# A graph layer's step on TensorE: counts of a slice ahead of placing, begun at group 28 instead of 31

## The chip, the cores and the metric

The kernel runs on one core of a Trainium2 chip. The metric is the device time of one execution in microseconds (us), the median of several runs. Five engines work side by side from queues of their own: TensorE (PE, with its weight loads as PEld), VectorE (DVE), ScalarE (ACT), GpSimd (POOL) and SyncE (SP, which issues DMAs).

## The reference

One layer of a graph network over 12500 nodes of 256 features, with 200000 edges sorted by their destination:

```
h   = relu(layernorm(x))                       # 12500 x 256
agg = segment_sum(h[src], dst)                 # 200000 edges
z   = (1 + eps_gin) * h + agg
t   = relu(batchnorm(z @ W1 + b1, g1, bt1))    # 12500 x 512
out = x + relu(batchnorm(t @ W2 + b2 + h, g2, bt2))
```

## The kernel before, in words

The edges are cut into tiles of 128 and the tiles into 131 groups of 12 (`GT`). One iteration of the loop at L951 is a *step* and belongs to one group; 126 steps run there, the last five groups after it. What a step does:

- **Fetching.** POOL's `gather` (L592) issues 12 indirect DMAs, each fetching the 128 source rows of a tile, four groups ahead of the sums that read them. There are four buffers, so the gather of a group waits until the sums of the fourth fetched group before it have been read. Groups below `LEAD` = 30 fetch rows of `x`, and their layer norm is done on the fly: `look` on DVE (L477), `scale` on DVE (L496, L498), `relus` on ACT (L504). Later groups fetch finished rows from `h_one`.
- **Summing.** DVE compares destinations with a ramp (`oh`, `edges`, L645) and PE's `sums` (L677) multiplies one-hot by rows, 12 tiles per group, two matmul records a tile in the trace. Two groups that follow each other share one PSUM tile (`ps`). `hold` (L731) copies a group's sum out as `zs` two steps later: on ACT below group 30, on DVE from there.
- **Placing.** PE's `put` (L744) spreads the sum of group i-3 to its columns; it writes a PSUM tile `pz2` from the pool `ps_z`, which has two. DVE's `add` (L759) of group i-4 adds such a tile to `zc` and so frees it.
- **Slices.** When a chunk of 512 nodes is complete, the first product follows in four *slices*, one a step: PE's `slice_of` (L769). With `apart` its result goes into `ps_z` too, so that places and slices take the two tiles in turn; without, into another pool (`next_ph`). In the next step `take` reads it on DVE (L780), copies it (L786: ACT up to step 30, then DVE), and sends it to `t_tab`.
- **Counting.** Ten groups (`COUNTED`: 41, 50, ..., 122) are not fetched. For each, the sum over its edges is made from all of `h` and a matrix of counts, in 13 *strips*: DVE marks (`mark`, L868, one step ahead, with an SP DMA of 1 MB of `h_one`, L874), PE counts (`count_of`: `count`, L887, 12 bf16 matmuls, and ACT's copy L899), and PE's `weigh` (L917, 8 matmuls) multiplies the strip before by its rows. `prepare` (L847 on) makes what the marks need, once, at the end of the step before `BEGIN`. The table `plan` gives one or two of the 130 strips to each step from `BEGIN` on: after n such steps int(`RATE` * n) strips are done.

Order on each engine is the order in which the code is written (a manual schedule); the framework adds semaphores where tiles are reused. In a step PE's list `works` is spread evenly between the 12 tiles of the sums. At a counted step, which has no sums, the list runs by itself.

Of the kernel before, what the change touches and what calls it, by code (L numbers as in the profile page):

```python
# [23 lines left out]
LEAD = 30  # L24
# [5 lines left out]
COUNTED = tuple(range(41, 131, 9))  # L30
WINDOWS = 4
BLOCKS = 8
BEGIN = 31
RATE = 1.6


COPIES = 2
# [6 lines left out]
def kernel(  # L44
# [23 lines left out]
    NCH = -(-N // CH)  # L68
# [86 lines left out]
    def slot(ga, t):  # L155
        return slots(ga, t)[:, 0, :]
# [231 lines left out]
    def fast():  # L388
# [24 lines left out]
        with ExitStack() as fs:  # L413
# [15 lines left out]
            with ExitStack() as es:  # L429
# [99 lines left out]
                def look_chunk(g):  # L529
                    look(((0, R, xts[g]),), -(-len(parts[g]) // 2), "c", g)  # L530
# [74 lines left out]
                def wait_for(i, eng):  # L605

                    if i in arrival:
                        eng.wait_ge(*arrival.pop(i))
                        return True
# [44 lines left out]
                def sum_place(i):  # L654
                    if not halves:
                        pair = ps_s.tile([P, 2, D], F32, name="ps")
                        halves.extend((pair[:, 1, :], pair[:, 0, :]))
                    return halves.pop()

                def sums(i, among=()):  # L660

                    if i in COUNTED:
                        for work in among:
                            work()
                        return
                    t0, n = groups[i]
                    ga, oh = gathered.pop(i), ohs.pop(i)
                    waited = wait_for(i, nc.tensor)
                    ps = sum_place(i)
                    order = list(reversed(range(n)))  # L670
                    at = {(k + 1) * n // (len(among) + 1): work for k, work in enumerate(among)}
                    for k, j in enumerate(order):
                        if k in at:
                            at[k]()
                        rows = left if t0 + j == full_tiles else P
                        lhsT, rhs = oh[:rows, j, :], slot(ga, j)[:rows]
                        part = nc.tensor.matmul(ps, lhsT=lhsT, rhs=rhs, start=(j == order[0]), stop=(j == order[-1]))  # L677
                        if waited:
                            behind(i, part)
                            waited = False  # L680
                    summed[i] = ps
# [79 lines left out]
                def slice_of(c, f, apart=False):  # L761

                    n = chunks[c][1] * R
                    if apart or c == NCH - 1 and f >= 2:
                        ph = ps_z.tile([P, DC, WIDE], F32, name="pz2").rearrange("p d w -> p (d w)")
                    else:
                        ph = next_ph()
                    for d in range(DC):
                        nc.tensor.matmul(  # L769
                            ph[:, :n], lhsT=w1s[:, d, f * P : (f + 1) * P],  # L770
                            rhs=zc[c][:, d, :n], start=(d == 0), stop=(d == DC - 1),
                        )
                    slices[c, f] = ph
                    if f == HC - 1:
                        del zc[c]
# [50 lines left out]
                plan, strips, turns_of = {}, [(k, s) for k in range(NC) for s in range(NS)], 0  # L826
                for i in range(BEGIN, NG - CLOSE):
                    if i not in COUNTED:
                        turns_of += 1
                        upto = min(int(turns_of * RATE), len(strips))  # L830
                        done = sum(len(v) for v in plan.values())
# [119 lines left out]
                for i in range(NG - CLOSE):  # L951
                    before = added
                    if next_of(i) is not None:
                        gather(next_of(i))
                    if 0 < i <= NCH:
                        turn(i - 1)
                    if i + 1 < LEAD:
                        scale("g", i + 1)
                    if i < NCH:
                        scale("c", i)  # L960
                    edges(i + FRONT)
                    if i >= 2:
                        spots(i - 2)
                        hold(i - 2)
                    if i + 1 < LEAD:
                        relus(gathered[i + 1], GT, gathered[i + 1], "g", i + 1)
                    if i < NCH:
                        h_chunk(i)
                    if i + 2 < LEAD:
                        look(gathered[i + 2], GT // 2, "g", i + 2)  # L970
                        root("g", i + 2)
                    if i + 1 < NCH:
                        look_chunk(i + 1)
                        root("c", i + 1)
                    for c, f in taken:
                        if i > LEAD:
                            take(c, f, nc.vector.tensor_copy, nc.sync)
                        else:
                            take(c, f)
                    while added <= i - 4:  # L980
                        add(added)
                        added += 1
                    if 0 < i <= NCH:
                        turn_out(i - 1)
                    if i < NCH:
                        h_rows(i)
                    for c in scales.get(i, ()):
                        z_scale(c)

                    def puts():  # L990
                        if i >= 3:
                            put(i - 3)

                    while last(whole) < before:
                        queue += [(whole, f) for f in range(HC)]
                        whole += 1
                    taken = queue[:1]
                    queue = queue[1:]

                    def slice_ups():  # L1000
                        for c, f in taken:
                            slice_of(c, f, i >= LEAD)

                    works = [puts, slice_ups]
                    for one in plan.get(i, ()):
                        works.append(functools.partial(count_of, *one))
                        if strips.index(one):
                            works.append(functools.partial(weigh, *strips[strips.index(one) - 1]))
                        if one == strips[-1]:
                            works.append(functools.partial(weigh, *one))  # L1010
                    sums(i, works)
                    if i + 1 == BEGIN:
                        prepare()
                    for one in plan.get(i + 1, ()):
                        mark(*one)
                    for c in loads.get(i, ()):
                        z_load(c)
# [604 lines left out]
```

## Time and profile before

| | |
|---|---|
| median of 3 runs | 2024.14 us (2023.56 to 2026.66) |
| the profiled execution | 2024.22 us, span 2022.4 us |
| mean granted TensorE clock | 0.952 |
| PE busy | 1779.5 us (88%) |
| DVE busy | 1259.6 us (62%) |
| ACT busy | 569.5 us (28%) |
| POOL busy | 1440.0 us (71%) |
| DMA | 462.70 MB, mean 229 GB/s |

A timeline row gives the start of a run of like instructions and its length, the engine, the line, what is written and read, and in brackets the idle time of the engine ahead of it with what ended it. Matmuls overlap a little, so the length of a piece of PE work is best read from its start to the start of the next. PEclk is the granted clock of TensorE, 1.00 being full.

### The profile page before, as it was taken

The page shows a single profiled execution, that of the slowest core. Times are in us where ns is not written, and L with a number is a line of the kernel's source. Part 1 is how long each engine was busy: PE and PEld are TensorE (multiplying, and loading weights), DVE is VectorE, ACT ScalarE, POOL GpSimd, SP SyncE. Part 2 cuts the span into 40 slices and gives each one's busy share as a digit, 9 for nine tenths or more (in the row PEclk, how much of TensorE's full clock was granted, in tenths as well). Part 3 has the DMA queues.
Part 4 walks back from the last instruction along what each step waited for, and adds up shares of the span by engine and source line. Part 5 has one row for each costly group of instructions (what it writes and reads, how often), then busy time and mean ns, then how long its engine had stood idle before and what let it go on. Part 6 is the DMA issues. An engine that isn't in the chain of part 4 may idle for free.

```text
span 2022.4 us, 22287 instructions
## 1 busy us (share of the span) xinstructions
PE 1779.5 (88%) x8138; PEld 1388.9 (69%) x8138; DVE 1259.6 (62%) x1488; ACT 569.5 (28%) x1049; POOL 1440.0 (71%) x1489
## 2 busy tenths in 40 slices
PE   2566667677999999999999999999999999999997
PEld 2455455456788888778788778877878888764445
DVE  5565665747556656665656747647566466337997
ACT  4566666652111111111111111111111111015545
POOL 7777777777777777777777777777776777773540
PEclk9777888888999999999999999999999999999999
DMA  6667677665667677676766767767666676558898
GB/s 191 198 217 225 217 231 245 190 215 149 220 220 237 231 226 239 221 248 227 239 225 220 250 220 231 237 221 238 221 222 222 214 242 230 152 181 285 302 332 324
DMA packets 159094, 462.70 MB, mean 229 GB/s; under 512 B 30868, under 2 KB 58684, under 8 KB 143614
## 3 DMA queue, kind: packets, MB, share of 16 engines
q1 hardware_dynamic: 85001, 264.39, 38.1%
q0 software_dynamic: 69248, 189.16, 30.8%
q10 hardware_dynamic: 4724, 7.61, 1.1%
q8 instruction: 66, 1.08, 0.2%
q14 instruction: 55, 0.44, 0.1%
HBM read 397.00 MB, written 64.05 MB: 228 GB/s over the span
## 4 chain that ended last, share of the span: by engine, by line
PE 69%; DVE 12%; DMA 8%; POOL 3%; issue 3%; ACT 3%; SPq 0%; ACTq 0%; DVEq 0%; POOLq 0%
PE ps L677 22%; PE ph L917 20%; PE ph L887 8%; PE pz L769 6%; PE pz L744 5%; DVE stg L477 4%; DMA gta<-in_x_dram,srcT 3%; POOL gt L592 2%; PE one L1161 2%; DMA gt<-in_x_dram,srcT 2%; DMA more<-in_x_dram,srcT 2%; PE pr L1161 2%; PE pq L1161 2%; PE ph L769 1%; DVE stc L477 1%
## 5 line engine op out<-in xcount | busy, mean ns | idle before, releaser
L592 POOL DMA_INDIRECT gt<-h_one,srcT x1083 | 1023.7, 945 | 338.6 <-issue 324.7
L677 PE MATMUL ps<-gt,oh 128*128 128x256 f32 x2424 | 615.1, 387 | 16.6 <-DMA gt<-h_one,srcT 9.5
L677 PEld LDWEIGHTS ps<-gt,oh 128*128 128x128 f32 x2424 | 461.2, 195 | 116.1 <-issue 44.0
L868 DVE TENSOR_TENSOR more<-col,more 128x3072 bf16<-128x3072 f32 (+1 forms) x130 | 410.0, 3165 | 77.0 <-PE ph L887 76.9
L899 ACT COPY more<-ph 128x512 f32<-128x512 f32 (+1 forms) x260 | 144.8, 561 | 1089.1 <-PE ph L887 1070.8
L917 PE MATMUL ph<-gta,more 128*128 128x256 f32 x1308 | 296.5, 379 | 0.0
L917 PEld LDWEIGHTS ph<-gta,more 128*128 128x128 f32 x1308 | 248.5, 190 | 33.8
L731 DVE COPY zs<-ps 128x256 f32<-128x256 f32 x89 | 37.1, 417 | 370.8 <-PE ps L677 370.8
L645 DVE TENSOR_TENSOR oh<-col,dstT 128x1536 f32<-128x1536 f32 x119 | 208.0, 1749 | 32.4 <-PE ps L677 32.4
L887 PE MATMUL ph<-more,more 128*128 128x256 bf16 (+1 forms) x1560 | 181.9, 266 | 0.0
L744 PE MATMUL pz<-at,zs 128*128 128x256 f32 x476 | 133.4, 405 | 43.8 <-DVE ts L786 27.6
L887 PEld LDWEIGHTS <-more 128*128 128x128 bf16 x1560 | 145.7, 98 | 32.3
L592 POOL DMA_INDIRECT gt<-in_x_dram,srcT x144 | 136.1, 945 | 43.9 <-issue 17.7
L917 PE MATMUL ph<-more,more 128*128 128x256 f32 x652 | 147.7, 379 | 0.0
L744 PEld LDWEIGHTS pz<-at,zs 128*128 128x128 f32 x476 | 93.2, 202 | 70.5 <-DVE ts L786 38.8
L769 PE MATMUL pz<-zc,w1s 128*128 128x512 f32 (+1 forms) x296 | 137.0, 586 | 0.0
L917 PEld LDWEIGHTS ph<-more,more 128*128 128x128 f32 x652 | 123.9, 190 | 16.8
L769 PE MATMUL ph<-zc,w1s 128*128 128x512 f32 (+1 forms) x104 | 61.5, 730 | 43.4 <-ACT ts L786 28.6
L759 DVE TENSOR_TENSOR zc<-pz,zc 128x512 f32<-128x512 f32 (+7 forms) x185 | 91.0, 516 | 6.1 <-PE pz L744 6.1
L592 POOL DMA_INDIRECT gta<-in_x_dram,srcT x80 | 75.6, 945 | 24.4 <-issue 10.1
L477 DVE BATCH_NORM_STATS2 stg<-gt 128x6 f32<-128x512 f32 x72 | 45.6, 688 | 64.5 <-DMA gt<-in_x_dram,srcT 64.0
L592 POOL DMA_INDIRECT more<-in_x_dram,srcT x72 | 68.0, 945 | 21.9 <-issue 7.3
(228 smaller groups left out, 1812.3 us busy)
## 6 DMA issues: line engine op xcount, KB each, us to landing
gta<-h_one SPq DMA_DIRECT2D x80, 1024.0 KB
more<-h_one SPq DMA_DIRECT2D x40, 1024.0 KB
t_tab<-ts SPq DMA_DIRECT2D x71, 256.0 KB
gt<-h_one,srcT POOLq DMA_INDIRECT x1083, 3.6
h_cols<-gt SPq DMA_DIRECT2D x24, 512.0 KB
zc<-h_cols SPq DMA_DIRECT2D x24, 512.0 KB
yT<-h_cols SPq DMA_DIRECT2D x24, 512.0 KB
gt<-in_x_dram SPq DMA_DIRECT2D x18, 512.0 KB
```

The costliest lines, as they stand in the source:

```text
L477: reader = nc.vector.bn_stats(st[:, c : c + 2, :].rearrange("p c s -> p (c s)"), two.rearrange("p c d -> p d c"),)
L592: fetch = nc.gpsimd.indirect_dma_start(out=slot(ga, t - t0)[:rows], out_offset=None, in_=x if i < LEAD else h_one, in_offset=bass.Indirect ...
L645: nc.vector.tensor_tensor(oh, col[:, :P].unsqueeze(1).to_broadcast([P, n, P]), dstT[:, t0 : t0 + n].unsqueeze(2).to_broadcast([P, n, P]), ...
L677: part = nc.tensor.matmul(ps, lhsT=lhsT, rhs=rhs, start=(j == order[0]), stop=(j == order[-1]))
L744: nc.tensor.matmul(pz[:, d, :n], lhsT=zs[:, d * P : (d + 1) * P], rhs=at[:, :n], start=True, stop=True)
L759: nc.vector.tensor_add(side, pz[:, :, a - lo : b - lo], side)
L769: nc.tensor.matmul(ph[:, :n], lhsT=w1s[:, d, f * P : (f + 1) * P], rhs=zc[c][:, d, :n], start=(d == 0), stop=(d == DC - 1),)
L868: nc.vector.tensor_tensor(marks[(k * NS + s) % 3][:, :, :n], col[:, :n].unsqueeze(1).to_broadcast([P, GT, n]), keys[k % 2][:, s, :].unsque ...
L887: nc.tensor.matmul(ph[:, w * strip : w * strip + n], lhsT=low[:, j, :], rhs=marked[:, j, :n], start=(t == 0), stop=(t == WT - 1),)
L899: nc.scalar.copy(to[:, :b, 2 * v * WD : 2 * (v + 1) * WD].rearrange("p a (w d) -> p w a d", w=2), ph.rearrange("p (w a d) -> p w a d", w=2 ...
L917: nc.tensor.matmul(total, lhsT=counts[m % 2][:, a, :], rhs=nodes_of[m % 3][:, a, :], start=(s == 0 and a == 0), stop=(s == NS - 1 and a == ...
L1161: nc.tensor.matmul(ps, lhsT=w[:, k, :], rhs=t[:, k, :], start=(k == 0), stop=(k == DC - 1))
```

## The change

`BEGIN` goes from 31 to 28 and `RATE` from 1.6 to 1.55: the 130 strips lie over the steps 28 to 120 (84 of them) and not 31 to 121 (82). In a step with strips, `works` was puts, slice, count, weigh (, count, weigh) and becomes count, puts, weigh, slice (, count, weigh). Steps without strips keep puts, slice. The slices of the steps 26 to 29 take a tile of `ps_z` (`apart` from step 26 on and not from step 30 on).

```diff
-BEGIN = 31
-RATE = 1.6
+BEGIN = 28
+RATE = 1.55
...
                     def slice_ups():
                         for c, f in taken:
-                            slice_of(c, f, i >= LEAD)
-
-                    works = [puts, slice_ups]
+                            slice_of(c, f, i > NCH)
+
+                    works, others = [], [puts, slice_ups]
                     for one in plan.get(i, ()):
                         works.append(functools.partial(count_of, *one))
+                        works += others[:1]
                         if strips.index(one):
                             works.append(functools.partial(weigh, *strips[strips.index(one) - 1]))
+                        works += others[1:]
+                        others = []
                         if one == strips[-1]:
                             works.append(functools.partial(weigh, *one))
+                    works += others
                     sums(i, works)
                     if i + 1 == BEGIN:
                         prepare()
```

`NCH` is 25. PE's order in steps 26 and 27 (`ps_2798` holds the sums of groups 26 and 27, `pz2_2740` the place of group 22, `pz2_2803` that of 23, `pz2_2871` that of 24). Before:

```order
L744 MATMUL pz2_2803<-at_2701,zs_2703 128x256 x2
L677 MATMUL ps_2798<-gta1_81,oh_2617 128x256 x4
L769 MATMUL ph_2810<-zc_1642,w1s_85 128x512 x2
L677 MATMUL ps_2798<-gta1_81,oh_2617 128x256 x4
L677 MATMUL ps_2798<-gt_313,oh_2699 128x256 x4
L744 MATMUL pz2_2871<-at_2770,zs_2772 128x256 x2
L677 MATMUL ps_2798<-gt_313,oh_2699 128x256 x4
L769 MATMUL ph_2878<-zc_1642,w1s_85 128x512 x2
```

The same engine and steps, now:

```order
L744 MATMUL pz2_2803<-at_2701,zs_2703 128x256 x2
L677 MATMUL ps_2798<-gta1_81,oh_2617 128x256 x4
L769 MATMUL pz2_2810<-zc_1642,w1s_85 128x512 x2
L677 MATMUL ps_2798<-gta1_81,oh_2617 128x256 x4
L677 MATMUL ps_2798<-gt_313,oh_2699 128x256 x4
L744 MATMUL pz2_2871<-at_2770,zs_2772 128x256 x2
L677 MATMUL ps_2798<-gt_313,oh_2699 128x256 x4
L769 MATMUL pz2_2878<-zc_1642,w1s_85 128x512 x2
```

Nothing moved in time here; the two slices take their turn among the two tiles of `ps_z`, between the places of groups 23, 24 and 25.

PE's order around the counted group 50, from the place of group 46 in step 49 to the first tile of group 51 (the strip's count, 24 rows, left out by the cut ahead of it). Before, the part of step 49 ahead of the count:

```order
L744 MATMUL pz2_4489<-at_4391,zs_4393 128x256 x2
L677 MATMUL ps_4486<-gt_4120,oh_4323 128x256 x2
L769 MATMUL pz2_4494<-zc_3358,w1s_85 128x512 x2
L677 MATMUL ps_4486<-gt_4120,oh_4323 128x256 x3
L887 LDWEIGHTS more3_318
```

Now, the part of step 49 behind the count, and step 50 (the place of group 47 and a slice):

```order
L744 MATMUL pz2_4612<-at_4491,zs_4493 128x256 x2
L677 MATMUL ps_4591<-gt_4224,oh_4400 128x256 x3
L917 MATMUL ph_4434<-gta0_79,more3_318 128x256 x8
L677 MATMUL ps_4591<-gt_4224,oh_4400 128x256 x2
L769 MATMUL pz2_4628<-zc_3462,w1s_85 128x512 x2
L677 MATMUL ps_4591<-gt_4224,oh_4400 128x256 x3
L744 MATMUL pz2_4645<-at_4581,zs_4583 128x256 x2
L769 MATMUL pz2_4648<-zc_3462,w1s_85 128x512 x2
L677 MATMUL ps_4591<-gt_4323,oh_4579 128x256
```

The slice of step 49 stood ahead of the count and the weighing and stands behind them now, three tiles from the end of the step. Groups 49 and 51 share the PSUM tile `ps_4591`.

DVE's order over the same steps, now (before it is the same with other numbers): it takes that slice (`pz2_4628`), adds, marks two strips for step 51, compares for group 53, and only then holds group 49 (`zs_4674`), which reads the shared tile.

```order
L780 BN_STATS st1_257<-pz2_4628 128x6
L786 COPY ts_4641<-pz2_4628 128x512
L759 TENSOR_TENSOR zc_3881<-pz2_4612,zc_3881 128x2x256
L868 TENSOR_TENSOR more0_315<-col_321,more3_318 128x3072
L868 TENSOR_TENSOR more1_316<-col_321,more3_318 128x3072
L645 TENSOR_TENSOR oh_4670<-col_321,dstT_70 128x1536
L736 TENSOR_SCALAR at_4672<-col_321,shift_71 128x256
L731 COPY zs_4674<-ps_4591 128x256
```

## The prediction

> **What bounds the kernel now.** I read the groups first, then the waits of POOL and of PE, then single steps of the timeline. The group of the fetches in the loop:
>
> ```profile
> L592 POOL DMA_INDIRECT gt<-h_one,srcT x1083 | 1023.7, 945 | 338.6 <-issue 324.7
> ```
>
> POOL needs 0.945 us for a fetch and 0.30 to the next: 1.25 us a tile, 15.0 us a group, and nearly all its idle time is its own issuing. So POOL keeps a timetable, and PE can only make it late. Where does it? POOL's waits from 1500 to 1815 us, and the first of them:
>
> ```profile
> POOL gt L592 <- PE ps L677: 10.0, 4, 4.0
> ```
> ```profile
> 1521.21 0.94 POOL L592 DMA_INDIRECT gt<-h_one,srcT  x1 [3.29 <-PE ps L677]
> ```
>
> Four waits for the sums that free a buffer. Each has 0.30 of issuing in it, so POOL loses 10.0 - 1.2 = 8.8 us to PE; nothing that only makes PE quicker is worth more than these, and a little at the end. PE's own waits from step 33 to group 106 (519 to 1533 us):
>
> ```profile
> PE pz L744 <- DVE ts L786: 21.9, 23, 1.3
> PE ps L677 <- DVE zs L731: 6.9, 2, 4.1
> ```
>
> The place waits for DVE's copy of the last slice, since both use the two tiles of `ps_z` in turn. One stretch of PE's timeline (group 49's step, the counted 50, the start of 51) prices the pieces, start to start, and DVE's beside it shows the chain on which a counted step hangs:
>
> ```profile
> 749.35 1.88 PE L769 MATMUL pz<-zc,w1s 128*128 128x512 f32 x4
> 751.06 1.46 PE L677 MATMUL ps<-gt,oh 128*128 128x256 f32 x6
> 752.36 1.47 PE L887 MATMUL ph<-more,more 128*128 128x256 bf16 x12
> 753.67 1.03 PE L677 MATMUL ps<-gt,oh 128*128 128x256 f32 x4
> 754.53 3.62 PE L917 MATMUL ph<-more,more 128*128 128x256 f32 x16
> 757.99 1.46 PE L677 MATMUL ps<-gt,oh 128*128 128x256 f32 x6
> 759.28 1.03 PE L744 MATMUL pz<-at,zs 128*128 128x256 f32 x4
> 760.14 1.88 PE L769 MATMUL pz<-zc,w1s 128*128 128x512 f32 x4
> 762.12 0.70 PE L677 MATMUL ps<-gt,oh 128*128 128x256 f32 x2
> ```
> ```profile
> 751.26 0.70 DVE L780 BATCH_NORM_STATS2 st<-pz 128x6 f32<-128x512 f32 x1 [0.82 <-PE pz L769]
> 751.88 0.67 DVE L786 COPY ts<-pz 128x512 f32<-128x512 f32 x1
> ...
> 753.07 6.61 DVE L868 TENSOR_TENSOR more<-col,more 128x3072 bf16<-128x3072 f32 x2
> 759.59 1.75 DVE L645 TENSOR_TENSOR oh<-col,dstT 128x1536 f32<-128x1536 f32 x1
> ...
> 761.65 0.41 DVE L731 COPY zs<-ps 128x256 f32<-128x256 f32 x1
> ```
>
> A tile costs 0.433 (three from 751.06 to 752.36), a group 5.2, a slice 1.71, a count 1.31, a weighing 3.46, a place 0.86. From 519.15 to 1533.73 PE has 66 groups, 74 places, 56 slices, 105 counts (8 of them of a strip a quarter as wide, for which I take a third) and 99 weighings: 975.3 us. The stretch lasts 1014.6, so 39.3 us are waits and the restarts behind them; the two rows of waits make 28.8 of that.
>
> **The change, part by part.** PE's work is the same in sum; only its place in time moves. The question is how late PE is against POOL's timetable at its tightest groups.
>
> *Slices of steps 26 to 29 in `ps_z`.* They have to wait for DVE's adds, and these stand behind `look`, which waits for fetched rows:
>
> ```profile
> 448.73 2.07 PE L744 MATMUL pz<-at,zs 128*128 128x256 f32 x4 [9.89 <-DVE zc L759]
> ...
> 484.93 2.93 PE L677 MATMUL ps<-gt,oh 128*128 128x256 f32 x6 [4.66 <-DMA gt<-h_one,srcT]
> ...
> 500.09 0.67 PE L677 MATMUL ps<-gt,oh 128*128 128x256 f32 x2 [4.86 <-DMA gt<-h_one,srcT]
> ...
> 518.28 1.89 PE L677 MATMUL ps<-gt,oh 128*128 128x256 f32 x8
> ```
> ```profile
> 448.00 0.68 DVE L759 TENSOR_TENSOR zc<-pz,zc 128x512 f32<-128x512 f32 x1
> ...
> 459.37 0.67 DVE L759 TENSOR_TENSOR zc<-pz,zc 128x512 f32<-128x512 f32 x1
> ...
> 473.80 0.16 DVE L847 TENSOR_SCALAR offsets<-col 128x13 f32<-128x13 f32 x1
> ...
> 477.48 3.35 DVE L868 TENSOR_TENSOR more<-col,more 128x3072 bf16<-128x3072 f32 x1
> ```
>
> Before, place 24 alone waited, until 448.73. Now the slice of step 26 takes the tile that the add of 448.00 frees (448.7), and place 24 the one of the add of 459.37 (460.1). From 448.7: slice, eight tiles, 2 us of restart (below): 456; wait to 460.1; place, eight tiles, slice, restart: step 27 ends at 468.0, not 456.9, some 11 us later. `prepare` and the first mark (473.80 to 480.83, 7.0 us) come behind the add of 459.37, so the first count is ready at 467, in time.
>
> *Counting from 28 on.* Steps 28 to 32 hold 5 groups and places (30.3), 3 slices (5.1), 7 counts (9.2) and 6 weighings (20.7), and about 1.2 of small waits for DVE and ACT: step 33 starts at 534.5. Before it was two tiles after 518.28, 519.15. PE is 15.4 us behind there, with 4 strips (19.1 us) done ahead; the two waits for fetched rows (9.5) are filled with work. The fetch of group 33 needs the sums of 29, which end at 495.6; it is due at 498.4, so POOL isn't late yet. The strips' loads of 1 MB on SP's queue move ahead with the marks; the third takes the buffer of group 28's rows, free when its sums end near 477, and is needed by the weighing in step 30, near 500: I cost them at nothing, and a late one at the few us by which it is late.
>
> *Counts ahead of places.* DVE holds, takes the statistics and copies the slice in 0.4 + 0.6 + 0.7, some 1.75 us after a step starts. The place now stands behind a count and three or four tiles, 2.6 to 3.0 us. So its wait goes, and so do the two for `zs`, whose stretch is laid out anew: -39.3 to group 106, and over the shorter way to group 61 (917.35 - 519.15 = 398.2, pieces 384.4) -13.8.
>
> *A new wait at counted steps.* The two groups around a counted one share a PSUM tile, so the sums of 51 wait until DVE has held 49: behind the take of the slice, an add, two marks and a comparison. From the end of that slice (751.06) to the end of the hold (762.06) this takes 11.0 us. Before, the slice stood ahead of the count, and PE had just as much to do. Now three tiles, a place and a slice are left behind it: 3.9 us. PE waits 7.1 us at the four places where one strip and a slice come ahead and two strips behind (50, 59, 77, 104), and some 2 at 95, where no slice stands. Where two strips come ahead (41, 68, 86, 113), 8.2 us of PE's work is behind the slice, against 11.0 - 3.26 (one mark less) = 7.75: no wait, by 0.5.
>
> *The restart.* Behind waits of over 4 us the granted clock (PEclk, the third column from the right) is half:
>
> ```profile
> 448.70:450.60 1.90, 1.87 (x5) 1.51 (x6) 1.87 (x4) 1.90 (x4) 1.60 (x2) 0.50 0.47 129
> 450.60:452.40 1.80, 1.80 (x6) 1.44 (x5) 0.47 (x2) 1.80 (x5) 1.19 (x3) 0.50 0.26 82
> 485.00:487.60 2.60, 2.60 (x6) 2.11 (x7) 2.60 (x2) 0.00 (x0) 1.99 (x3) 0.50 0.35 106
> 487.60:489.40 1.80, 1.80 (x6) 1.39 (x5) 1.80 (x1) 0.00 (x0) 1.44 (x2) 0.50 0.47 137
> 1365.00:1369.00 4.00, 4.00 (x24) 3.55 (x22) 4.00 (x2) 2.58 (x4) 3.09 (x4) 1.00 0.93 332
> 1375.00:1377.70 2.70, 2.70 (x7) 2.11 (x7) 2.66 (x1) 0.00 (x0) 2.09 (x3) 0.50 0.48 152
> ```
>
> Half a clock for 3.7, 4.4 and 2.7 us loses 1.85, 2.2 and 1.35 and a little at the edges: I take 2.1, so a new wait costs 9.2, four 36.8. The Trainium skill (TensorE: Matmul & The Clock Gate, Part 1: The HAM clock gate) says that after an idle window of about 3.4 us the array runs at half rate until it has been busy for about as long. That is 1.7 for each wait, an estimate; the sum would be 1.6 us lower by it, and the 0.50 in these rows agrees with its half rate.
>
> **The sum.** Ends of sums beside the fetches that need their buffers (61 and 65, 106 and 110):
>
> ```profile
> 917.35 1.03 PE L744 MATMUL pz<-at,more 128*128 128x256 f32 x4
> ```
> ```profile
> 933.32 0.94 POOL L592 DMA_INDIRECT gt<-h_one,srcT  x1 [0.30 <-issue]
> ```
> ```profile
> 1533.73 1.03 PE L744 MATMUL pz<-at,more 128*128 128x256 f32 x4
> ```
> ```profile
> 1536.22 0.95 POOL L592 DMA_INDIRECT gt<-h_one,srcT  x1 [0.30 <-issue]
> ```
>
> At 61 PE has 933.32 - 917.35 = 16.0 to spare. The strips done ahead are still 4 there (int(1.55*31) = 48 against int(1.6*28) = 44), so PE is later by 15.4 - 13.8 + 2*9.2 = 20.0: POOL loses 4.0. At 106 POOL without its wait of 3.0 at 1521.21 would be 0.5 ahead of PE; the strips ahead have shrunk from 4 to 2 (-9.5), so PE is later by 15.4 - 9.5 - 39.3 + 2.0 + 36.8 = 5.4, and POOL has lost 5.9 in all. Behind 113 PE runs ahead. At the end, the sums of 128 wait for their rows no more than these take:
>
> ```profile
> 497.15 0.95 POOL L592 DMA_INDIRECT gt<-h_one,srcT  x1 [0.31 <-issue]
> ```
> ```profile
> 1795.78 0.95 POOL L592 DMA_INDIRECT gt<-h_one,srcT  x1 [0.30 <-issue]
> ```
> ```profile
> 1800.35 5.34 PE L677 MATMUL ps<-gt,oh 128*128 128x256 f32 x24
> ```
>
> The last fetch of group 32 (497.15) let PE start at 500.09, 2.9 later; so those of 128 are there at 1798.7, and PE, early now, gains 1.6. POOL's loss falls from 8.8 to 5.9: 2024.2 (the profiled execution, 0.1 above the median) - 2.9 - 1.6 = 2019.7.
>
> **Rivals.** *POOL is never late.* If the new waits cost less (a DVE chain 1.3 us shorter, or waits under the length that halves the clock), 5.9 goes to nothing: 2024.2 - 8.8 - 1.6 = 2013.8. For it: every step of the sum is an upper bound where DVE finds time early. Against it: the chain of 11.0 stands in the rows above. By the page's 1.7 it would still be 4.3 late.
>
> *PE starts counting too late and nothing is won.* If step 33 starts at 540, because the places of steps 27 to 29 wait longer behind `look` and `prepare` than I allow, POOL loses 5.5 more: 2025.2. For it: the margin at group 33's fetch is 2.8 us, and three engines meet there.
>
> *Slower: the counted steps cost more than the places did.* If DVE's chain is 2 us longer there (a mark that waits for its buffer), four waits grow to 9.1 and those at 41, 68 and 86, with 0.5 to spare, open to 1.5: 12.5 more by group 106, 2032. It decides from 1.4 us on (8.5 more, 2028.2). The same end comes if the places keep their waits, so that the change doesn't do what it says: group 61 would then be 13.8 later, 2033. Against both: DVE is idle for 0.82 ahead of 751.26 and the count gives it 2.6 us.
>
> **The numbers.** A measurement here tells 0.2% (4.05 us) from no change: under 2020.1 is faster, over 2028.2 slower. Forecast 0.45, spread over 2016 to 2023 by the price of the restart and of the early steps (0.26 of it under 2020.1); POOL never late 0.18; too late a start 0.22; slower 0.15. So faster 0.44, same 0.41, slower 0.15. The range of 2014 to 2026.5 leaves out the slower case and the edges; the forecast's own is 2016 to 2023.
>
> **What would show it.** Places without waits from 519 on; waits of about 7 us of `ps` for DVE's `zs` ahead of groups 51, 60, 78 and 105 with a clock of 0.5 behind them; step 27 ending near 468 and step 33 starting near 534.5; POOL's waits for `ps` near groups 64, 65 and 110, some 6 us together, and none behind 1600. POOL waiting already at group 33 would prove me wrong, and so would a PE wait in every step.

## The result and the profile after

The changed kernel takes 2029.11 us (median of 21 runs, 2025.9 to 2032.35), the kernel before 2024.74 (21 runs). The ratio, that of the two means and so a little smaller than that of the medians, is 1.0017 with an interval of 1.0011 to 1.0023: slower, by a little less than 0.2%. The forecast was 2019.7. The profiled execution took 2029.49 us (span 2027.7, clock 0.943), 5.3 us more than the one of before.

PE's waits from 519 to 1745 us show both halves of the change. The row of places waiting for `ts` (21.9 us to group 106 before) is gone; in its place stands one of sums waiting for `zs`:

```profile
PE ps L677 <- DVE zs L731: 29.5, 5, 6.7
```

One of them, ahead of group 51, on PE's timeline and on DVE's:

```profile
770.28 1.88 PE L769 MATMUL pz<-zc,w1s 128*128 128x512 f32 x4
778.82 1.22 PE L677 MATMUL ps<-gt,oh 128*128 128x256 f32 x2 [6.66 <-DVE zs L731]
779.83 2.77 PE L887 MATMUL ph<-more,more 128*128 128x256 bf16 x12
```
```profile
767.97 0.70 DVE L780 BATCH_NORM_STATS2 st<-pz 128x6 f32<-128x512 f32 x1 [6.63 <-PE pz L769]
...
769.77 6.61 DVE L868 TENSOR_TENSOR more<-col,more 128x3072 bf16<-128x3072 f32 x2
776.30 1.75 DVE L645 TENSOR_TENSOR oh<-col,dstT 128x1536 f32<-128x1536 f32 x1
777.96 0.47 DVE L736 TENSOR_SCALAR at<-col,shift 128x256 f32<-128x256 f32 x1
778.35 0.41 DVE L731 COPY zs<-ps 128x256 f32<-128x256 f32 x1
```

DVE first idles 6.63 us for the slice, which comes late now, and then PE idles 6.66 us for DVE. The count behind the wait takes 2.77 us instead of 1.47: the windows of that place have half the clock (PEclk is the third number from the right).

```profile
778.90:781.00 2.10, 2.10 (x8) 1.42 (x9) 2.10 (x5) 0.00 (x0) 1.54 (x2) 0.50 1.00 384
781.00:783.00 2.00, 2.00 (x10) 1.54 (x9) 2.00 (x1) 0.89 (x2) 1.39 (x3) 0.50 1.01 281
```

What it costs is read on POOL, whose waits of more than its 0.30 of issuing are these:

```profile
498.98 0.94 POOL L592 DMA_INDIRECT gt<-h_one,srcT  x1 [0.99 <-ACT zs L731]
...
922.93 0.94 POOL L592 DMA_INDIRECT gt<-h_one,srcT  x1 [4.08 <-PE ps L677]
...
940.23 0.94 POOL L592 DMA_INDIRECT gt<-h_one,srcT  x1 [2.60 <-PE ps L677]
...
1165.87 0.94 POOL L592 DMA_INDIRECT gt<-h_one,srcT  x1 [0.97 <-PE ps L677]
...
1528.16 0.94 POOL L592 DMA_INDIRECT gt<-h_one,srcT  x1 [2.65 <-PE ps L677]
...
1545.45 0.94 POOL L592 DMA_INDIRECT gt<-h_one,srcT  x1 [2.63 <-PE ps L677]
```

Less 0.30 each they make 12.1 us, against 8.8 before: 3.3 us more lost on POOL. They are the fetches of groups 33, 64, 65, 82, 109 and 110; before, POOL had no such wait ahead of group 109.

At the end, PE is early and waits for the rows of group 128, and then runs at half clock (the last row is the place in the profile of before):

```profile
1801.95 8.37 PE L677 MATMUL ps<-gt,oh 128*128 128x256 f32 x24 [5.08 <-DMA gt<-h_one,srcT]
1810.84 1.13 PE L744 MATMUL pz<-at,zs 128*128 128x256 f32 x4 [0.52 <-DVE zs L731]
```
```profile
1804.00:1806.00 2.00, 2.00 (x7) 1.53 (x6) 0.00 (x0) 0.00 (x0) 1.53 (x2) 0.50 0.35 90
```
```profile
1806.21 1.13 PE L744 MATMUL pz<-at,zs 128*128 128x256 f32 x4 [0.52 <-DVE zs L731]
```

From the start of these sums to the place behind them it is 8.9 us, 5.9 before (1800.35 to 1806.21). Place 127 behind them starts 4.6 us later than before: 3.4 from POOL (its last fetch starts at 1817.9 against 1814.5) and 1.2 more, where I had foreseen a gain of 1.6. The rest of the 5.3 us, 0.7, is a longer wait in the second product (2.3 instead of 1.5 us, ahead of 1853.78).

### The profile page after: what moved, and what is told of

Read it like the earlier page. It is cut to its first block, busy times and chain, and to the rows that moved or that the text cites. A ratio compares the mean times of both kernels' runs of the same rounds, so it can differ in the third digit from the quotient of the medians.

```text
span 2027.7 us, 22267 instructions
## 1 busy us (share of the span) xinstructions
PE 1781.7 (88%) x8138; PEld 1395.0 (69%) x8138; DVE 1256.7 (62%) x1488; ACT 569.3 (28%) x1049; POOL 1441.3 (71%) x1489
## 4 chain that ended last, share of the span: by engine, by line
PE 63%; DVE 10%; POOL 10%; DMA 7%; issue 5%; ACT 4%; SPq 0%; ACTq 0%; POOLq 0%; DVEq 0%
PE ps L677 21%; PE ph L917 19%; POOL gt L592 8%; PE ph L887 7%; PE pz L769 5%; DVE stg L477 4%; PE pz L744 4%; DMA gt<-in_x_dram,srcT 3%; PE one L1165 2%; DMA gta<-in_x_dram,srcT 2%; PE pr L1165 2%; PE pq L1165 2%; DMA more<-in_x_dram,srcT 1%; DVE more L868 1%; DVE stc L477 1%
## 5 line engine op out<-in xcount | busy, mean ns | idle before, releaser
L887 PE MATMUL ph<-more,more 128*128 128x256 bf16 (+1 forms) x1560 | 188.2, 272 | 0.0
L769 PE MATMUL pz<-zc,w1s 128*128 128x512 f32 (+1 forms) x312 | 146.5, 593 | 11.5 <-DVE zc L759 10.8
L780 DVE BATCH_NORM_STATS2 st<-pz 128x6 f32<-128x512 f32 x76 | 52.7, 694 | 146.5 <-PE pz L769 146.2
L769 PE MATMUL ph<-zc,w1s 128*128 128x512 f32 (+1 forms) x88 | 54.6, 763 | 48.6 <-ACT ts L786 31.6
L769 PEld LDWEIGHTS pz<-zc,w1s 128*128 128x128 f32 x312 | 59.5, 192 | 53.1 <-issue 36.9
```

The source lines that it names most:

```text
L769: nc.tensor.matmul(ph[:, :n], lhsT=w1s[:, d, f * P : (f + 1) * P], rhs=zc[c][:, d, :n], start=(d == 0), stop=(d == DC - 1),)
L887: nc.tensor.matmul(ph[:, w * strip : w * strip + n], lhsT=low[:, j, :], rhs=marked[:, j, :n], start=(t == 0), stop=(t == WT - 1),)
```

## The experiments

The theory going in: the time is POOL's timetable plus the moments at which PE makes it late. The new order takes 1.1 to 1.55 us from each of some twenty steps and gives back 7 to 9 us at each counted step where the slice now comes too late for DVE's chain, of which 2 to 2.5 us are the clock. The rival: the stall at the beginning (slices of steps 26 to 29) sets PE's lateness. Each ratio below is to the kernel before, run in between on the same chip. Step lengths, waits and POOL's losses are those of the one profiled execution of each kernel; in six of the kernels (`begin_alone`, `apart_28`, `hold_early`, the two `mix` kernels and `slice_mid`) it is the longest of its runs. Six runs, the last of this section, give no answer.

**order_alone: the new order by itself.** `BEGIN` = 31, `RATE` = 1.6 and `slice_of(c, f, i >= LEAD)` as before; `works` as in the changed kernel.

> The new order of the works with counting from step 31 at 1.6 strips and slices before step 30 left where they were. Theory (the time is POOL's timetable plus what PE makes it wait; the new order drops the waits of places but opens a wait of 6.7 us and a cold restart of some 2.6 us at counted steps with one strip ahead and two behind): PE starts step 33 at 519 as before, the new waits stand ahead of groups 51, 60 and 105, shorter ones (about 3 us) ahead of 69 and 114, the old one of 4 ahead of 96; POOL loses about 3.6 us near groups 105 to 119 and none before; with a restart of 3 us at group 128 the time is about 2020, 0.2% under before. Rival (the order itself costs: the count ahead of the place delays what DVE and ACT need): POOL loses 10 us or more, time above 2025.

Ratio 1.0006 (0.9996 to 1.0015): no change; profiled 2026.04 us. The waits are where they were foreseen, ahead of 51, 60, 69, 96, 105 and 114:

```profile
PE ps L677 <- DVE zs L731: 31.6, 6, 6.7
```

POOL loses 12.1 us, 6.65 of them at group 109, where I had said 3.6 in all and a time near 2020; the median is 2026.58. By its numbers the rival came true (10 us or more, over 2025). The size was wrong to the same side as the forecast: at the start of group 106's sums PE is 3.6 us later than before. Whether the count ahead of the place costs this, as the rival says, or the late slice, is settled by `slice_mid` below. What the steps show is that the order pays and takes within the same kernel: step 45 is 1.55 us shorter than before, step 49 with the counted 50 is 5.9 longer and step 51 1.8.

**begin_alone: the earlier begin by itself.** The changed kernel with

```diff
-                    works, others = [], [puts, slice_ups]
+                    works = [puts, slice_ups]
...
```

that is, the loop of before: puts, slice, count, weigh.

> Counting from step 28 at 1.55 and slices of steps 26 to 29 in the pool of two, with the old order (puts, slice, count, weigh). Theory: the early stall stays (step 33 starts near 537 to 540, not 519), the waits of places stay, no wait of 6.7 us at counted steps except those of 4 and 3 us that before had at 96 and 105; PE is late by about 18 to 20 us less the strips done ahead, POOL loses 9 to 12 us, spread from group 61 on: time 2026 to 2030. Rival (the early start is what helps and the order is what hurts): POOL loses less than 5 us, time under 2020.

Ratio 0.998 (0.9971 to 0.9989), 2023.27 us: faster, where 2026 to 2030 was foreseen, and not the rival's 2020 either. The early stall is there, larger than I said, and it is nearly the only wait that POOL has:

```profile
505.31 0.94 POOL L592 DMA_INDIRECT gt<-h_one,srcT  x1 [6.28 <-ACT zs L731]
```

The profile's releaser is ACT's hold at 504.61; the fetch of group 33 waits for the sums of 29, which end a little ahead of it. Behind, POOL loses only 0.2 us, though the places still wait for `ts` (25.0 us, 27 times, from 519 to 1745). So four strips done ahead are worth a little more than the early stall costs, and a kernel that was to be late by 18 to 20 us less those strips recovers. The same steps with the two orders, in this kernel and the changed one, show the price of the order without any difference in the plan (step length in us, the counted step that follows included):

| step | old order | new order | difference |
|---|---|---|---|
| 45 | 17.96 | 16.41 | -1.55 |
| 54 | 13.64 | 12.53 | -1.11 |
| 49 (and 50) | 16.48 | 22.29 | +5.81 |
| 51 | 18.25 | 19.87 | +1.62 |
| 58 (and 59) | 15.36 | 22.29 | +6.93 |
| 76 (and 77) | 16.54 | 22.35 | +5.81 |
| 103 (and 104) | 16.55 | 22.35 | +5.80 |

**mix_28 and mix_31: the new order except ahead of a counted step.** With the changed plan (`mix_28_again`) and with the plan and slices of before (`mix_31_again`):

```diff
                     works, others = [], [puts, slice_ups]
+                    if i + 1 in COUNTED:
+                        works, others = others, []
```

> The changed kernel, but the step ahead of a counted one keeps the old order (puts, slice, count, weigh); the run before it fell into a stretch in which the kernel before took 2450 us. Theory: the four waits of 6.7 us and their half clock go (some 35 us of PE time by group 106), the waits of places stay away; POOL waits 0.7 to 2 us at group 33 for the early stall and nowhere behind it; with a restart at group 128 the time is 2017 to 2019. Rival (POOL's lateness is set by the early steps): POOL still waits 5 us or more behind group 60, time above 2023.

> The kernel before, counting from 31 at 1.6, with the new order except in the step ahead of a counted one. Theory: no wait of 6.7 us, some 20 us of place waits gone, so PE is early by more than the 8.8 us that POOL lost before: POOL loses nothing, time 2017 to 2018 with the restart at group 128. Rival (counts first delay the takes, and other waits come instead): POOL loses 4 us or more, time 2021 to 2025.

Ratios 0.9948 (0.9935 to 0.9962) and 0.995 (0.9937 to 0.9964): both about 0.5% faster than before, 2016.0 and 2015.75 us, a little under the 2017 to 2019 foreseen. These two beat both kernels. In `mix_28` step 49 takes 16.48 us again, and 51, 60, 78 and 105 take 17.40, 17.40, 15.68 and 15.68 where the changed kernel has 19.87, 18.97, 18.33 and 17.87. PE in `mix_28` now waits more for rows than for DVE (519 to 1745 us):

```profile
PE ps L677 <- DMA gt<-h_one,srcT: 12.7, 4, 6.9
PE pz L744 <- DVE ts L786: 6.0, 6, 1.3
PE ps L677 <- DVE zs L731: 1.9, 3, 1.6
```

In `mix_31` the two waits for `zs` that the kernel before has at 96 and 105 stay (6.9 us). POOL loses 0.4 us in the one and nothing in the other. That the two take the same time settles the rival: with the early stall (`mix_28`: step 33 at 538.3) and without it (`mix_31`: 519.2) the time is the same, to the 0.14% that five runs tell, once the counted steps are mended. Beside that order, no gain of the earlier begin and the slices in `ps_z` shows.

**slice_mid: is it the count ahead of the place, or the slice behind the weighing?** The changed kernel; in the step ahead of a counted one the slice stands directly behind the places, the count still first.

```diff
                         works.append(functools.partial(count_of, *one))
-                        works += others[:1]
+                        works += others if i + 1 in COUNTED else others[:1]
...
-                        works += others[1:]
+                        works += [] if i + 1 in COUNTED else others[1:]
```

> The changed kernel, but in the step ahead of a counted one the order is count, puts, slice, weigh: the count still comes first, only the slice moves ahead of the weighing. Theory (the wait is DVE's chain of 11 us from the end of that slice, less PE's work behind it): five tiles, a weighing, a place and a slice (8.2 us) are left behind the slice instead of 3.9, so the waits ahead of groups 51, 60, 78 and 105 shrink from 6.7 to about 2.5 us, with little or no half clock behind them: 5 to 6 us less at each, POOL loses under 1.5 us, time 2015 to 2019. Rival (a count ahead of the place is what opens the wait): the waits stay at 6 us or more and the time at 2027 or more.

Ratio 0.9964 (0.9951 to 0.9978), 2017.94 us. The waits shrink as worked out, to 2.7:

```profile
774.61 1.22 PE L677 MATMUL ps<-gt,oh 128*128 128x256 f32 x2 [2.71 <-DVE zs L731]
```

POOL loses nothing. So it is the place of the slice, and not the count ahead of the place. One thing was not as foreseen: the half clock stays behind three of the four waits. Behind two waits of the same length, 2.77 us, it is half once and full once:

```profile
1133.20:1136.00 2.80, 2.80 (x11) 1.92 (x12) 2.80 (x5) 0.30 (x1) 2.03 (x3) 0.50 1.02 394
1492.00:1494.00 2.00, 2.00 (x16) 1.70 (x17) 2.00 (x5) 0.59 (x1) 1.70 (x2) 1.00 0.88 314
```

Step 78 is 3.0 us longer than with a full clock (15.68 us in `mix_28`), step 105 as long as there. Steps 51 and 60, behind waits of 2.71 and 2.70 us, are 1.4 and 1.5 us longer.

**warm_waits: the clock's share.** The changed kernel with work of no use in the four waits:

```diff
                     sums(i, works)
+                    if i in (50, 59, 77, 104):
+                        filler = ps_t.tile([P, CH], F32, name="ph")
+                        for _ in range(14):
+                            nc.tensor.matmul(filler[:, :D], lhsT=w1s[:, 0, :P], rhs=w1s[:, 0, :D], start=True, stop=True)
```

> The changed kernel with 14 matmuls into a tile that nobody reads at the end of the counted steps 50, 59, 77 and 104, some 6.1 us of work of no use in each of the four waits. Theory (half clock behind the wait is a part of its cost): groups 51, 60, 78 and 105 start when they did, but their steps last 17.4, 17.4, 15.7 and 15.7 us instead of 19.9, 19.0, 18.3 and 17.9, 8.9 us less in sum; POOL loses some 4 to 7 us less than in the changed kernel, time 2023 to 2025.5. Rival (the clock is a sign and not a cost, since DVE's chain sets the steps): the steps keep their lengths and the time stays at 2027 or more.

Ratio 0.9972 (0.9961 to 0.9983), 2018.58 us: adding 56 matmuls that nobody reads makes the changed kernel about 9 us faster, and faster than before. Group 51 again:

```profile
771.08 6.21 PE L1020 MATMUL ph<-w1s 128*128 128x256 f32 x28
777.91 0.70 PE L678 MATMUL ps<-gt,oh 128*128 128x256 f32 x2 [0.62 <-DVE zs L732]
778.45 1.47 PE L888 MATMUL ph<-more,more 128*128 128x256 bf16 x12
```
```profile
778.00:780.00 2.00, 2.00 (x16) 1.71 (x17) 2.00 (x5) 0.58 (x1) 1.49 (x2) 1.00 1.02 395
```

The sums of 51 start within 1 us of where they did, the count takes 1.47 and the clock is 1.00. The four steps last 17.40, 17.40, 15.68 and 15.68 us, as foreseen, 8.9 us less in sum. POOL loses 2.6 us instead of 12.1: nearly all of the 8.9 reached POOL (0.9 us of the 9.5 are an earlier step 33, at 536.1), where I had foreseen a half to three quarters. So the time lies under the 2023 to 2025.5 foreseen.

**warm_tail: the end.** The same filler (10 matmuls, 4.3 us) ahead of the sums of group 128 of the changed kernel, `if i == NG - 3`.

> The changed kernel with 10 matmuls into a tile that nobody reads (4.3 us) ahead of the sums of group 128, where PE waits 5.1 us for fetched rows and then takes 8.9 us to the next group instead of 6.8. Theory (at the end an early PE pays the half clock, so that the gain foreseen for the end is a loss): the sums of 128 start when they did and last 5.3 instead of 8.4 us; everything behind is 2 to 3 us earlier, time 2025 to 2027 where the changed kernel takes 2028 to 2029. Rival (POOL alone sets the end, and the restart is hidden by the pieces behind it): the step of 128 is shorter and the end stays where it was.

```profile
1797.85 4.48 PE L1078 MATMUL ph<-w1s 128*128 128x256 f32 x20
1803.05 5.45 PE L678 MATMUL ps<-gt,oh 128*128 128x256 f32 x24 [0.73 <-DMA gt<-h_one,srcT]
1809.02 1.13 PE L745 MATMUL pz<-at,zs 128*128 128x256 f32 x4 [0.52 <-DVE zs L732]
```

The step takes 6.0 instead of 8.9 us, and the profiled execution is 2.9 us shorter (2026.58 against 2029.49) although POOL lost 13.1 us in it, 1.0 more. Against the kernel before, the place behind these sums now stands 2.8 us later and POOL's last fetch 4.5 (1818.98), so at the end PE gains 1.7 us on POOL; with the half clock it lost 1.2. The timed ratio, 1.0014 (1.0005 to 1.0023), overlaps that of the changed kernel, and the median, 2028.33, lies over the 2025 to 2027 foreseen, so that the gain is shown in the trace alone and not in the time.

**apart_28: the early stall.** Slices of steps 26 and 27 back in the other pool.

```diff
-                            slice_of(c, f, i > NCH)
+                            slice_of(c, f, i >= BEGIN)
```

> The changed kernel, with the slices of steps 26 and 27 back in the other pool; those of 28 and 29 stay in the pool of two. Theory: the wait of 10.8 us of the slice of step 26 goes, but counting can begin only when prepare and the first mark are done, near 467 to 470, so step 28 waits for its first count instead and step 33 starts 2 to 4 us earlier than in the changed kernel (533 to 535 against 537): POOL loses 2 to 4 us less, time 2025 to 2027. Rival (the whole 11 us of the early stall comes back): step 33 starts at 526 to 528, POOL loses less than 3 us, time 2018 to 2021.

Both the theory and the rival missed. Ratio 1.0035 (1.0021 to 1.0049), if anything slower than the changed kernel, and step 33 starts at 539.7, later than its 537.0. The stall moves to the first count, which waits for `prepare` and its mark, and the second half of the same count (a count is two tiles of 6 matmuls) waits once more:

```profile
468.11 1.44 PE L887 MATMUL ph<-more,more 128*128 128x256 bf16 x6 [8.71 <-DVE more L868]
474.95 1.44 PE L887 MATMUL ph<-more,more 128*128 128x256 bf16 x6 [5.41 <-ACT ts L786]
```

The first was worked out, the second wasn't: the wait that went from the slice came back behind ACT's copy. The halves of a count and the slices outside `ps_z` take their `ph` from the same pool of two, `ps_t`, and the copy that empties one (474.34) stands on ACT behind the twelve `relus` of group 29 (468.43, 6.0 us). POOL loses 10.1 us, 2.0 less than in the changed kernel, as the theory said; that the time is not shorter goes with POOL's slower pace in this profile (last section). Counting from 28 stalls the early steps with the slices in either pool.

**hold_early: a repair that wasn't one.** The changed kernel, with `spots(i - 1)` and `hold(i - 1)` moved from the step behind a counted one into the counted step, ahead of the marks.

```diff
-                    if i >= 2:
+                    if i >= 2 and i - 1 not in COUNTED:
                         spots(i - 2)
                         hold(i - 2)
...
+                    if i in COUNTED:
+                        spots(i - 1)
+                        hold(i - 1)
```

> The changed kernel, with DVE holding the group ahead of a counted one in the counted step itself, ahead of the marks (its spots and hold move from the next step to this one); nothing else moves. Theory: the waits of 6.7 us ahead of groups 51, 60, 78 and 105 and the half clock behind them go, about 37 us of PE time by group 106; the stall at the start stays (step 33 at 537), POOL loses about 0.7 us at group 33 and nothing behind it; PE is early at the end and pays the restart at group 128: time about 2017 to 2018. Rival (the lateness comes from the early steps, and the counted steps only show it): the waits go but POOL still loses 5 us or more, time above 2022.

Ratio 1.0003 (0.9994 to 1.0012), 2027.75 us against 2017 to 2018 foreseen. The waits for `zs` go, but two others come:

```profile
PE pz L744 <- DVE ts L786: 16.1, 6, 3.8
PE ph L887 <- DVE more L868: 12.7, 9, 2.5
```

In step 51 place 48 waits 3.77 us, because the take of the counted step's slice stands behind the two marks on DVE, and counts wait for marks that come later now. POOL loses 14.3 us. By its numbers the rival came true (5 us or more, above 2022), but not by its cause: what makes PE late are the new waits at the counted steps, not the early ones. The wait was moved along DVE's queue; in the `mix` kernels, where the slice comes earlier, it goes.

**begin_30: an earlier begin without the stall.** The kernel before with `BEGIN` = 30 and `RATE` = 1.57.

> The kernel before with counting from step 30 at 1.57, and nothing else. Theory: one strip goes into the two waits for fetched rows at groups 31 and 32, step 33 still starts near 519, and PE is up to 5 us earlier behind it: POOL loses about 4 us instead of 8.8, near groups 112 to 124; time 2019.5 to 2022. Rival (only an early stall comes of it): POOL waits at group 33 or 34, time 2024 or more.

Ratio 0.9977 (0.9965 to 0.9988), 2020.65 us, as foreseen, but in part by luck: POOL loses nothing rather than 4 us, and in this profile its pace is 4.4 us slower by the end (last section). Step 33 starts at 516.3, not 519.1: of the two waits for rows (4.66 and 4.86) one of 3.28 is left. So one step earlier is a gain, in place of the idle time at 31 and 32; that the stall takes what a begin at 28 adds to it fits the ratio of `begin_alone`, 0.998.

**Six runs without an answer.** They fell into two stretches in which the kernel before took 2418 to 2474 us. In their own profiles the granted clock is 0.86 to 0.89 and POOL waits 235 to 350 us for PE's sums, so it is not POOL's timetable that sets the time there; nothing is read from them for the question of this document. `mix_28`, `mix_30` and `warm_tail` were slower than the kernel before under these conditions, and why was not looked into. The first runs of the two `mix` kernels (ratios 1.0062 and 1.0025), of `begin_30` (1.0022 and 1.0019) and of `warm_tail` (1.035) stand above with their later ones; `mix_30`, the `mix` order with counting from step 30 at 1.57 (1.0093), was not run again and stays open.

> The changed kernel, but the step ahead of a counted one keeps the old order (puts, slice, count, weigh); all other steps keep the new one. Theory (the new order is good for 1.1 to 1.55 us at about 20 steps and bad by 7 to 9 us at the four steps ahead of groups 51, 60, 78 and 105, because the slice comes too late for DVE's chain there): the waits of 6.7 us go, the waits of places stay away, POOL waits 0.7 to 2 us at group 33 for the early stall and nowhere behind it; with a restart at group 128 the time is 2017 to 2019. Rival (POOL's lateness is set by the early steps): POOL still waits 5 us or more behind group 60, time above 2023.

> The kernel before (counting from 31 at 1.6, slices before step 30 as before) with the new order except in the step ahead of a counted one. Theory: no wait of 6.7 us, some 20 us of place waits gone, so PE is early by more than the 8.8 us that POOL lost before: POOL loses nothing, time 2017 to 2018 with the restart at group 128. Rival (an order with counts first delays the takes, and other waits come instead): POOL loses 4 us or more, time 2021 to 2025.

> The kernel before with counting from step 30 at 1.57, one step earlier, and nothing else. Theory: one strip goes into the two waits for fetched rows at groups 31 and 32, so step 33 still starts near 519 and PE is 4 to 5 us earlier everywhere behind: POOL loses 4 us instead of 8.8, near groups 112 to 124; time 2019.5 to 2021.5. Rival (only an early stall as in the run with the begin alone comes of it): POOL waits at group 33 or 34, time 2024 or more.

> Counting from step 30 at 1.57 together with the new order except in the step ahead of a counted one. Theory: POOL loses nothing, as with the same order from step 31, so the two take the same time: 2017 to 2018. Rival (each moves the time by itself): 3 to 5 us less than with step 31.

> The changed kernel with 10 matmuls into a tile that nobody reads (4.3 us) ahead of the sums of group 128, where PE waits 5.1 us for fetched rows and then takes 8.9 us to the next group instead of 6.8. Theory (at the end an early PE pays the half clock, so that the gain foreseen for the end is a loss): the sums of 128 start when they did and last 5.3 instead of 8.4 us; everything behind is 2 to 3 us earlier, time 2025 to 2027 where the changed kernel takes 2028 to 2029. Rival (POOL alone sets the end, and the restart is hidden by the pieces behind it): the step of 128 is shorter and the end stays where it was.

> The kernel before with counting from step 30 at 1.57, and nothing else; the run before it fell into a stretch in which the kernel before took 2450 us. Theory: one strip goes into the two waits for fetched rows at groups 31 and 32, step 33 still starts near 519, and PE is up to 5 us earlier behind it: POOL loses about 4 us instead of 8.8, near groups 112 to 124; time 2019.5 to 2022. Rival (only an early stall comes of it): POOL waits at group 33 or 34, time 2024 or more.

## Why the prediction was wrong

The mechanism held, place by place; the sum of its sizes did not.

- *What bounds the kernel.* Right: where POOL lost nothing (`mix_31`, `slice_mid`, `begin_30`) the kernel was faster than before, and what was lost on POOL and at the end gives the changed kernel's time. Over all profiles, the start of POOL's last fetch less what POOL lost is 1805.5 to 1806.1 us in seven and 1809.9 to 1810.6 in five, so it is a timetable with two paces (last section).
- *Slices of steps 26 to 29.* Step 27 was to end at 468.0 and ended at 470.7, with waits of 10.8 and 10.2 us; step 33 was to start at 534.5 and started at 537.0. POOL did wait at group 33, by 0.7, which the prediction had named as a sign against itself. The miss of 2.5 us begins with a term that the prediction put at nothing but for its own lateness: the strips' loads of 1 MB. The second of them needs the sums of 26, which end 13.7 us later now, so it moves from 437.14 to 450.87, among the last fetches of group 29. Their last row lands 5.4 us behind its fetch, not 2.7; DVE's `look` at these rows and the add behind it, which frees the tile for place 24, come 2.5 us later (461.90, not the 459.37 taken over from before). Before, and now:

```profile
437.14 0.32 SPq L874 DMA_DIRECT2D gta<-h_one  x1
455.01 3.84 DVE L477 BATCH_NORM_STATS2 stg<-gt 128x6 f32<-128x512 f32 x6 [3.94 <-DMA gt<-in_x_dram,srcT]
```
```profile
450.87 0.32 SPq L874 DMA_DIRECT2D gta<-h_one  x1
457.55 3.83 DVE L477 BATCH_NORM_STATS2 stg<-gt 128x6 f32<-128x512 f32 x6 [10.29 <-DMA gt<-in_x_dram,srcT]
```

- *Counts ahead of places.* Right: no place waits for `ts` any more. Priced with the pieces of the prediction, all steps from 33 to 106 but those of the new waits are within 0.6 us in sum of their pieces, so the 39.3 us went. (The rows at 917.35 and 1533.73, read as ends of sums, are places one tile into the next step; the 0.4 us cancel in the sum.)
- *The new wait.* Right at all four places: 6.66 to 6.73 us against 7.1. Priced by step, the four places cost 38.0 us rather than 36.8: 26.8 of waits, 8.9 of half clock and 2.4 at the edges of the pieces. The small one ahead of 96 was 2.7, and 1.7 of restart behind it that the prediction did not give it; with edges the place costs 4.6 us, not 2.0.
- *The restart.* 8.9 us for four (`warm_waits` and `mix_28`) against 8.4. With the 1.7 a wait, an estimate, that the prediction worked out from the Trainium skill (TensorE: Matmul & The Clock Gate, Part 1: The HAM clock gate) it would have been 6.8; the measurement, 1.6 to 2.7 us a wait, decides.
- *The sum.* This step failed. At group 106 PE was to be 5.4 us later than before; it was 11.7 (sums of 107 at 1545.01 against 1533.30). 2.5 us come from the early steps, 2.6 from the place at 96 and 1.2 from the four others. Each term was off by little, but all three to one side, and POOL pays what is left of a difference between two sums of 40 us. POOL lost 12.1 instead of 5.9: 6.2 us.
- *The end.* The step with the wrong sign. It took the gain of an early PE, 1.6 us, and left out that PE then waits and restarts at half clock, though the prediction had just priced that. Measured: 1.2 lost, 2.8 us from the forecast; with the wait filled (`warm_tail`) the 1.6 is there. With the 6.2 and 0.7 in the second product this is 9.7 of the 9.8 us between 2019.7 and the profiled 2029.5.
- *The rivals.* By its time "slower", 2028.2 and more, is the nearest, but its cause did not come: the four waits are a little shorter than forecast, none opened at 41, 68 and 86, and the places lost theirs. "PE starts counting too late", 2025.2, named the early steps alone; they brought less than half of what POOL lost beyond the forecast.

That the load delays the rows is read from the profiles, not from a run that moves the load alone. In the seven with the load at 451 to 453 us the last row of group 29 lands after 4.0 to 5.7 us, in the five with it at 437 to 439 after 2.7; there it is group 28's that takes 5.6 to 7.1, against 3.3 to 5.0.

Not settled: why `begin_alone`'s runs reach from 2016.2 to 2028.2 us. The profiled one is the longest of them; POOL's slower pace is in it, and 1.6 us of half clock behind a wait of 2.2 us in the second product (1850.85).

## What to carry to other kernels

When two engines hand work back and forth in a fixed order, look for the step in which the other one has the longest queue, and give it its input first there; an order that is better in twenty steps can lose all of it in four. Where an engine must wait more than two or three microseconds, price the wait with the slow restart behind it, at the end of the stage too, and where the gain hangs on a difference of two large sums, make the range as wide as the errors of both. A transfer that moves in time has a price too, in what lands beside it. Going back to the old order in the steps ahead of the counted ones alone made of a loss of 0.2% a gain of 0.5%; moving nothing but the slice there, a gain of 0.4%.

## What the runs showed of the hardware

- Matmuls that nobody reads, put into a wait of 6.7 us, shortened the steps behind it by 1.6 to 2.7 us each, by keeping the granted clock at 1.00. The clock can fall behind waits as short as 2.7 us, and need not: in `slice_mid` 0.50 behind one of 2.77, 1.00 behind another.
- POOL's pace has two values. From the first fetch of group 33 to that of group 110, less its waits, it takes 1034.8 to 1035.1 us in the profiles of before, after, `order_alone`, `hold_early`, `mix_31`, `warm_waits` and `warm_tail`, and 1037.3 to 1037.6 in those of `begin_alone`, `apart_28`, `mix_28`, `slice_mid` and `begin_30`, with the same instructions. A fetch itself takes 945.2 to 945.5 ns in the first and 948.0 to 948.2 in the others; by POOL's last fetch it is 4.4 us. It is not the kernel that decides: `mix_28`, `mix_31` and `begin_30` were each profiled with both values (first and later runs). What does was not found, and differences of 4 us between single profiles are not to be put down to an edit before POOL's pace is compared.
- Fetched rows land later beside a load of 1 MB: the last row of group 29 lands 4.0 to 5.7 us behind its fetch in the seven profiles with the load just ahead of it, and 2.7 us in the five without.
